# Layer 0's products as sums of seven block products, their sums in two PSUM banks or one, and the row of scores put in order by its transfer

## The chip, the cores and the metric

One core of a Trainium2 chip runs the whole program in one launch. The metric is device time in microseconds. The kernel before takes 2461.74 us, the median of three runs (2460.16 to 2461.83).

## The reference

32 independent graphs of 512 nodes with 256 features go through four graph-attention layers. Each layer normalises x, applies relu to get h, computes a 512x512 matrix of scores, masks it by the graph's adjacency, normalises its rows and mixes the nodes' values. Layer 0 is the one that the change rebuilds most:

```python
h = jnp.maximum(_layernorm(x, axis=-1), 0.0)
# layer 0
mask = jnp.where(dep_adjs == 1, 0.0, NEG).astype(inputs.dtype)
q = jnp.einsum('bnh,hk->bnk', inputs, att_W)
score = jnp.einsum('bnk,bmk->bnm', q, inputs) / jnp.sqrt(jnp.asarray(H, inputs.dtype))
att_adjs = jax.nn.softmax(score + mask, axis=-1)
x = inputs
for W, b in ((W0, b0), (W1, b1)):
    xw = jnp.einsum('bnh,hk->bnk', x, W) + b
    x = jnp.tanh(jnp.einsum('bnm,bmk->bnk', att_adjs, xw))
```

Layers 1 and 2 have scores that are a sum of one number per source and one per target node, through a leaky relu. Layer 3 has full scores again, formed from products of features. All data are float32.

## The kernel before, in words

Every graph is its own chain of operations; P is 128, a graph has NT = 4 tiles of 128 nodes, and features lie in HC = 2 halves of 128. Function `graph` lists the operations of one graph as planner entries: an engine (PE for TensorE, V for VectorE, A for ScalarE, G for GpSimd, D for the transfers on SyncE's queue), a planned cost (how long it holds its engine, and when its result is there), what it comes after, and the buffers that it uses. Class `Plan` then plays all entries of all 32 graphs and of the preparation forward in time. On each engine it takes the ready entry of the best rank, where earlier graphs come first with a distance `apart` between graphs; it tries 32 pairs of such distances and keeps the order that ends first by its own costs. That order is written out as the program, so every engine runs its list in order. An entry starts only when its buffers are free in the plan: 36 pages of SBUF, four value buffers, eight PSUM banks, and five slots, so that at most five graphs are in flight. A slot is taken at a graph's first code operation (L440) or statistics (L461), and is free after the output's store (L987).

Each layer starts with `normed`: statistics (L461, L462), a power on GpSimd (L468), the normalisation (L475), a split of the floats into two planes of 16 bits (L480), a transfer that transposes them (L483), and a copy that joins them into hT, features by nodes (L488).

Layer 0 then has features for all nodes (`features_t`, L513, two banks, evacuated at L517), the values (L682, bias added by L686), the scores (L696, four banks), their Exp straight out of PSUM (L700) and the mask (L703). `attend` (L662) multiplies the scores with the values for two tiles of nodes at a time, in two banks; the last column gives the row sums, of which L711 takes the reciprocal, and L714 applies tanh. L723 repeats the mixing with the result, L741 multiplies with W1, and L745 to L752 finish the layer.

Layers 1 and 2 take scores and values from one product (L596, evacuated by L600 and L603). The scores of the target nodes must become a row that every partition has. For the first and last five graphs TensorE turns them into a bank (L619). For the others `collect` (L624) writes them to DRAM as 128 lines of four numbers, and `spread` (L628) reads them back into a page, for all partitions. `leaky` (L635) adds the source's score and applies the leaky relu, and it reads the row with the two indices exchanged to undo the order in which `collect` wrote it. Exp follows (L639), then the mask (L764 or L791).

Layer 3 computes its features (L838), values (L855), scores (L878) and a further product (L855, for w) by function `seven`: a product of two-by-two blocks done with seven block products instead of eight. `block_sums` (L570) forms the four sums of blocks that some of the products take in place of plain blocks. The four results share partial sums: a bank is evacuated as one result (`write`), the next product is added on top of it in the same bank, the bank is evacuated again as the next result, and so on. The remaining products go to a second and third bank and are added to the results in SBUF (`add`). The weights' seven blocks are made once, by `seven_of`.

The softmax here doesn't subtract the row's maximum and nothing guards it: scores larger than these inputs give would overflow.

## Time and profile before

| | us |
|---|---|
| median of three runs | 2461.74 |
| the profiled execution, whole | 2461.46 |
| its span, first to last instruction | 2459.7 |
| PE busy in the window 401.20 to 2062.00 us | 1641.61 of 1660.80 |
| `row<-sd` to landing (median, 44 transfers) | 3.2 |
| DVE busy in the window 2400 to 2420 us | 19.42 of 20 |

The page's part 1 gives each engine's busy time. The busy time of PE counts pipelined passes from start to modelled end, so it says little on its own. Groups "by line" name the line of the kernel, the engine, the operation, the written and read tiles, the count, the busy time, the mean duration in ns, and the idle time before, with what ended most of it. Windows give busy time of each engine in a stretch. An f32 product is two passes on TensorE, and the counts are of passes.

### The profile page before, as it was taken

Reading aid. Unit: us, or ns where it says so; the run is one execution under the profiler, and the core shown is the slowest. Engines: PE = TensorE matmul, PEld = TensorE weight load, DVE = VectorE, ACT = ScalarE, POOL = GpSimd, SP = SyncE. Lnnn points to the kernel's source line nnn. Section 1 sums busy time; section 2 is a strip of 40 time slices with the busy share of each in tenths; the row PEclk is TensorE's granted clock in tenths of the full one; section 3 lists DMA queues with packets and bytes.
Section 4 is the critical chain, followed back from the end, with each engine's and each line's share of the span. In section 5 each row is a group of like instructions: output and inputs, shape, how many; then the busy total and the mean of one; then the engine's idle time right before and its main releaser. Section 6 shows DMA issues by size and latency. Waiting matters only on the chain.

```text
span 2459.7 us, 33966 instructions
## 1 busy us (share of the span) xinstructions
PE 2407.4 (98%) x10700; PEld 1877.3 (76%) x10700; DVE 1876.2 (76%) x5733; ACT 1742.8 (71%) x3233; POOL 253.8 (10%) x315
## 2 busy tenths in 40 slices
PE   7999999999999999999999999999999999999998
PEld 4678777777777777777777777777777777777877
DVE  5468878777777877787777777777777778756888
ACT  4466777767777777777677777777776777755884
POOL 2001001110010101011101101010011011100110
PEclk9999999999999999999999999999999999999999
DMA  7223333332333322333323333233333343321221
GB/s 178 46 56 82 73 69 82 82 74 54 80 76 82 82 64 64 80 80 82 71 54 81 74 82 82 64 65 80 80 76 70 62 83 81 71 46 22 44 46 41
DMA packets 437204, 175.92 MB, mean 72 GB/s; under 512 B 393408, under 2 KB 410432, under 8 KB 437024
## 3 DMA queue, kind: packets, MB, share of 16 engines
q1 hardware_dynamic: 430976, 154.34, 29.9%
q0 software_dynamic: 5360, 18.75, 2.3%
q8 instruction: 85, 1.39, 0.2%
q14 instruction: 95, 0.78, 0.1%
q10 hardware_dynamic: 688, 0.66, 0.1%
HBM read 64.49 MB, written 16.87 MB: 33 GB/s over the span
## 4 chain that ended last, share of the span: by engine, by line
PE 73%; ACT 17%; DVE 5%; issue 3%; DMA 2%; POOL 0%; SPq 0%; POOLq 0%; ACTq 0%; DVEq 0%
PE bank_a L662 28%; PE bank_v L596 9%; PE bank_z L723 9%; ACT e L635 8%; PE bank_o L741 4%; PE bank_f L513 4%; PE bank_f L838 4%; PE bank_w L855 4%; ACT e L639 3%; PE bank_q L696 3%; PE bank_v L855 3%; PE bank_s L878 3%; ACT xn L475 2%; PE bank_v L682 2%; ACT e L700 1%
## 5 line engine op out<-in xcount | busy, mean ns | idle before, releaser
L662 PE MATMUL bank_a<-v,e 128*128 128x257 f32 (+1 forms) x4096 | 978.0, 381 | 21.8 <-ACT y L714 17.5
L662 PEld LDWEIGHTS bank_a<-v,e 128*128 128x128 f32 x4096 | 757.9, 190 | 199.9 <-issue 68.6
L488 ACT COPY hT<-planesT 128x512 uint16<-128x512 uint16 x512 | 383.2, 767 | 42.1 <-DMA planesT<-planes 41.7
L468 POOL TENSOR_TENSOR rstd<-ve,mhalf 128x2 f32<-128x2 f32 x256 | 215.2, 849 | 1891.7 <-DVE ve L465 1807.6
L475 ACT ACTIVATE xn<-x,off,rstd 128x256 f32<-128x256 f32 x512 | 277.3, 593 | 123.1 <-DVE off L471 119.3
L596 PE MATMUL bank_v<-l_aug,hT 128*128 128x258 f32 x1024 | 251.5, 383 | 3.3 <-ACT r L807 1.7
L480 DVE COPY planes<-xn 128x512 uint16<-128x512 uint16 x512 | 207.9, 422 | 43.8 <-ACT xn L475 24.1
L723 PE MATMUL bank_z<-e,y 128*128 128x512 f32 x512 | 240.6, 592 | 0.0
L696 PE MATMUL bank_q<-fa,hT 128*128 128x512 f32 x512 | 239.3, 592 | 0.0
L596 PEld LDWEIGHTS bank_v<-l_aug,hT 128*128 128x128 f32 x1024 | 192.2, 191 | 35.5 <-issue 3.6
L461 DVE BATCH_NORM_STATS2 st<-x 128x6 f32<-128x256 f32 x512 | 209.0, 408 | 6.6 <-DMA x<-in_x_dram 6.6
L635 ACT ACTIVATE e<-row,sd 128x512 f32<-128x512 f32 x176 | 207.0, 1229 | 0.0
L603 ACT COPY v<-bank_v 128x256 f32<-128x256 f32 x256 | 92.9, 375 | 90.1 <-PE bank_v L596 75.8
L639 ACT ACTIVATE e<-e 128x512 f32<-128x512 f32 x256 | 151.9, 632 | 0.0
L696 PEld LDWEIGHTS bank_q<-fa,hT 128*128 128x128 f32 x512 | 94.9, 190 | 71.4 <-issue 60.8
L723 PEld LDWEIGHTS bank_z<-e,y 128*128 128x128 f32 x512 | 96.5, 190 | 69.1 <-issue 57.9
L885 DVE SCALAR_TENSOR_TENSOR e<-bank_s,v,mask 128x256 f32<-128x256 f32 x256 | 111.1, 476 | 16.5 <-PE bank_s L878 16.3
L682 PE MATMUL bank_v<-w_sb,hT 128*128 128x256 f32 x512 | 121.4, 380 | 0.0
L703 DVE TENSOR_TENSOR e<-e,mask 128x512 f32<-128x512 f32 x128 | 87.5, 688 | 44.0 <-ACT e L700 43.9
L741 PE MATMUL bank_o<-w_sb,zT 128*128 128x256 f32 x512 | 120.4, 379 | 0.0
L513 PE MATMUL bank_f<-hT,att_sb 128*128 128x512 f32 x256 | 119.8, 593 | 0.0
L682 PEld LDWEIGHTS bank_v<-w_sb,hT 128*128 128x128 f32 x512 | 97.1, 191 | 23.9 <-issue 6.1
(134 smaller groups left out, 3702.1 us busy)
## 6 DMA issues: line engine op xcount, KB each, us to landing
adj<-in_adj_dram SPq DMA_DIRECT2D x128, 256.0 KB, 2.9
x<-in_x_dram SPq DMA_DIRECT2D x32, 512.0 KB, 5.1
out_dram<-y POOLq DMA_DIRECT2D x32, 512.0 KB, 4.1
row<-row SPq DMA_DIRECT2D x44, 256.0 KB, 3.7
planesT<-planes SPq DMA_TRANSPOSE x512, 2.4
codeT<-code SPq DMA_TRANSPOSE x128, 2.6
crest<-crest SPq DMA_TRANSPOSE x64, 2.4
raw_w<-in_L_gnn_W_dram POOLq DMA_DIRECT2D x3, 256.0 KB, 7.1
```

Source lines behind the costliest of these rows:

```text
L468: nc.gpsimd.tensor_tensor(T[f"rstd{l}"][:, two(g)], T[f"ve{l}"][:, two(g)], mhalf[:, two(g)], ALU.pow)
L475: nc.scalar.activation(T[f"xn{l}"][:, t, :], T["x"][:, t, :], AF.Relu, bias=T[f"off{l}"][:, t : t + 1], scale=T[f"rstd{l}"][:, t : t + 1])
L488: nc.scalar.copy(bits[:, :, :, t * P : (t + 1) * P], T[f"planesT{l}_{t}"].rearrange("p (b c) n -> p b c n", b=2))
L513: nc.tensor.matmul(T[key], w_sb[:, c, k * P : (k + 1) * P], T[f"hT{l}"][:, c, :], start=(c == 0), stop=(c == HC - 1))
L596: nc.tensor.matmul(T[key][:, :cols], T[f"hT{l}"][:, c, t * P : (t + 1) * P], w_aug[:, c, :], start=(c == 0), stop=(c == HC - 1))
L635: nc.scalar.activation(e(l, c).rearrange("q (t p) -> q t p", t=NT), row, AF.Prelu, bias=T[f"sd{l}"][:, 1, c : c + 1], alpha=ALPHA)
L639: nc.scalar.activation(e(l, c), e(l, c), AF.Exp, scale=sign)
L662: nc.tensor.matmul(T[keys[j]][:, : LEAD + H + 1 - lead], e(l, c)[:, t * P : (t + 1) * P], T[f"v{l}"][:, c, lead:], start=(c == 0), stop=(c ...
L682: nc.tensor.matmul(T[key][:, j * H : (j + 1) * H], T["hT0"][:, c, t * P : (t + 1) * P], w0_sb[:, c, :], start=(c == 0), stop=(c == HC - 1))
L696: nc.tensor.matmul(T[key], T["hT0"][:, k, c * P : (c + 1) * P], T["fa0"][:, k, :], start=(k == 0), stop=(k == HC - 1))
L723: nc.tensor.matmul(T[f"bank_z{k}"], T["y0"][:, c, k * P : (k + 1) * P], e(0, c), start=(c == 0), stop=(c == NT - 1))
L741: nc.tensor.matmul(T[key][:, j * H : (j + 1) * H], T["zT"][:, k, t * P : (t + 1) * P], w1_sb[:, k, :], start=(k == 0), stop=(k == HC - 1))
```

## The change

Layer 0's three products (features, values, scores) go through `seven` as well. Its weights W0 and att_W are loaded into pages and turned into seven blocks by `seven_of`, as layer 3's are. `block_sums` forms hs0 from hT0, and fs0 from the features. Scores now come block by block: the block that is whole after one evacuation gets its Exp out of PSUM as before; the other three are copied out, get the further products added, and get their Exp in place.

`seven` itself, for layers 0 and 3, uses two banks instead of three, and one bank in two halves where a block product is at most 256 columns wide (`beside`: features and values of layer 0, features and w of layer 3). Its fifth product now waits for the fourth and for the addition of the second.

The row of scores of layers 1 and 2 is put in node order by `collect`, which writes single numbers to their places in DRAM, and L635 reads it straight. Planned costs change with it: 5000 in place of 3500 ns for `collect`'s landing, 629 in place of 570 ns for the leaky relu of the row out of SBUF, 334 in place of 395 and 602 in place of 640 for additions out of PSUM.

```diff
-V_SUM, V_INTO, V_BLOCK = (334.0, 425.0), (640.0, 730.0), (790.0, 880.0)
+V_SUM, V_BLOCK = (334.0, 425.0), (790.0, 880.0)
...
-D_OUT, D_SPREAD = (550.0, 3500.0), (550.0, 4500.0)
+D_OUT, D_SPREAD = (550.0, 5000.0), (550.0, 4500.0)
...
-    att_sb, w0_sb, w1_sb = (tile_of(n, H) for n in ("att_sb", "w0_sb", "w1_sb"))
-    l3_w1s, m3 = (tile_of(n, HALF, 7) for n in ("l3_w1s", "m3"))
+    w1_sb = tile_of("w1_sb", H)
+    att_s, w0_s, l3_w1s, m3 = (tile_of(n, HALF, 7) for n in ("att_s", "w0_s", "l3_w1s", "m3"))
...
-    nc.scalar.dma_start(out=w0_sb, in_=rows_of(w0))
-    nc.scalar.dma_start(out=att_sb, in_=rows_of(att_w))
+    w0_sb, att_sb = raw("raw9"), raw("raw10")
     nc.scalar.dma_start(out=b0_sb, in_=line_of(b0))
+    for n, dst, w, key in (("att", att_s, att_w, "raw10"), ("w0", w0_s, w0, "raw9")):
+        a = prepare("A", (500.0, 4000.0), [], lambda w=w, key=key: nc.scalar.dma_start(out=raw(key)(), in_=rows_of(w)), key)
+        ready[n] = seven_of(raw(key), dst, HALF, [a], key)
...
-        def features_t(l, hs, w_sb, ready):
...
-                key = f"bank_f{l}{k}"
-                def product(k, key):
-                    for c in range(HC):
-                        nc.tensor.matmul(T[key], w_sb[:, c, k * P : (k + 1) * P], T[f"hT{l}"][:, c, :],
-                                         start=(c == 0), stop=(c == HC - 1))
...
-                    nc.scalar.copy(T[f"fa{l}"][:, k, :], T[key])
...
-                a = op("PE", pe(n512=4), hs + ready, partial(product, k, key), key, f"hT{l}")
-                done.append(op("A", A_COPY, [a], partial(evacuate, k, key), key, f"fa{l}"))
...
-        def seven(key, cost, after, keys, work, write, add):
...
-            first = times(1, 0, True)
-            c11 = out(write, 0, 0, 0, first)
-            c12 = out(write, 0, 1, 0, times(6, 0, False, c11))
-            c22 = out(write, 1, 1, 0, times(7, 0, False, c12))
-            c21 = out(write, 1, 0, 0, times(4, 0, False, c22))
-            c11 = out(add, 0, 0, 1, times(2, 1, True, first), c11)
-            c22 = out(add, 1, 1, 2, times(5, 2, True, first), c22)
-            c12 = out(add, 0, 1, 2, times(3, 2, False, c22), c12)
+        def seven(key, cost, after, keys, work, write, add, beside=0):
...
+            p, q = f"bank_{key}p", f"bank_{key}{'p' if beside else 'q'}"
+            def times(x, bank, start, fresh, *wait):
+                return op("PE", cost, after(x) + list(wait), lambda: work(x, T[bank][:, start:], fresh), bank, *keys)
+            c11 = write(0, 0, p, 0, [times(1, p, 0, True)])
+            two = times(2, q, beside, not beside, c11)
+            c12 = write(0, 1, p, 0, [times(6, p, 0, False, c11)])
+            c22 = write(1, 1, p, 0, [times(7, p, 0, False, c12)])
+            four = times(4, p, 0, False, c22)
+            c21 = write(1, 0, p, 0, [four])
+            c11 = add(0, 0, q, beside, [two, c11])
+            c22 = add(1, 1, q, beside, [times(5, q, beside, True, four, c11), c22])
+            c12 = add(0, 1, q, beside, [times(3, q, beside, False, c22), c12])
             return {(0, 0): c11, (0, 1): c12, (1, 0): c21, (1, 1): c22}
...
-                line.append(dram.tile([P, NT], F32, tag=f"row_{T.places['slot']['number']}", name=f"row{l}_{b}"))
-                nc.sync.dma_start(out=line[0], in_=T[f"sd{l}"][:, 0, :])
+                line.append(dram.tile([N], F32, tag=f"row_{T.places['slot']['number']}", name=f"row{l}_{b}"))
+                nc.sync.dma_start(out=line[0].rearrange("(t p) -> p t", p=P), in_=T[f"sd{l}"][:, 0, :])
...
-                if turned:
-                    row = T[key].rearrange("q (t p) -> q t p", t=NT)
-                else:
-                    row = T[key][:, 0, :].rearrange("q (p t) -> q t p", t=NT)
-                nc.scalar.activation(e(l, c).rearrange("q (t p) -> q t p", t=NT), row, AF.Prelu,
-                                     bias=T[f"sd{l}"][:, 1, c : c + 1], alpha=ALPHA)
+                row = T[key] if turned else T[key][:, 0, :]
+                nc.scalar.activation(e(l, c), row, AF.Prelu, bias=T[f"sd{l}"][:, 1, c : c + 1], alpha=ALPHA)
...
-            ls = [op("A", A_PRELU, [a], partial(leaky, c), key, f"e{l}_{c // 2}") for c in range(NT)]
+            ls = [op("A", A_PRELU if turned else A_PRELU2, [a], partial(leaky, c), key, f"e{l}_{c // 2}") for c in range(NT)]
...
+        def features_t(l, right_after, right, w, ready, bias=None):
+            def work(x, p, fresh):
+                nc.tensor.matmul(p[:, : N // 2], w[:, x - 1, :], right(x), start=fresh, stop=True, skip_group_check=True)
...
+                def emit():
+                    if bias is None:
+                        nc.scalar.copy(block(i, l_), T[key][:, : N // 2])
+                    else:
+                        nc.scalar.activation(block(i, l_), T[key][:, : N // 2], AF.Identity, bias=bias[:, i : i + 1])
+                return op("A", A_HALF if bias is None else A_HALF_BIAS, after, emit, key, f"fa{l}")
...
+            def add(i, l_, key, start, after):
+                return op("V", V_SUM, after, lambda: nc.vector.tensor_tensor(
+                    block(i, l_), block(i, l_), T[key][:, start : start + N // 2], ALU.add), key, f"fa{l}")
+            done = seven(f"f{l}", pe(n256=2), lambda x: right_after(x) + ready, (f"hT{l}", f"hs{l}"), work, write, add,
+                         beside=N // 2)
+            return list(done.values())
...
-        qs = features_t(0, hs, att_sb, [])
-        vs = []
...
-            a = op("PE", pe(n256=8), hs[two(g)], partial(values, g, key), key, "hT0")
-            vs += [op("V", V_ADD, [a], partial(biased_v, g, j, key), key, "v0") for j in range(2)]
-        es = []
-        for c in range(NT):
...
-                    nc.tensor.matmul(T[key], T["hT0"][:, k, c * P : (c + 1) * P], T["fa0"][:, k, :],
-                                     start=(k == 0), stop=(k == HC - 1))
...
-                nc.scalar.activation(e(0, c), T[key], AF.Exp, scale=float(H) ** -0.5)
...
-            def masked0(c):
-                nc.vector.tensor_tensor(e(0, c), e(0, c), T["mask0"][:, c, :], ALU.mult)
-            a = op("PE", pe(n512=4), qs, partial(similar, c, key), key, "hT0", "fa0")
-            a = op("A", A_COPY, [a], partial(exp0, c, key), key, f"e0_{c // 2}")
-            es.append(op("V", V_MASK, [a, m0], partial(masked0, c), "mask0", f"e0_{c // 2}"))
+        right_after, right = block_sums("hs0", "hT0", lambda j, l, T=T: T["hT0"][:, j, half(l)], hs, left=False)
+        qs = features_t(0, right_after, right, att_s, ready["att"])
...
+        def write_v0(i, l, key, start, after):
+            return op("V", V_SUM, after, lambda: nc.vector.tensor_tensor(
+                block_v0(i, l), two_tiles(key, start, HALF),
+                b0_sb[:, i * HALF : (i + 1) * HALF].unsqueeze(1).to_broadcast([P, 2, HALF]), ALU.add), key, "v0")
+        def add_v0(i, l, key, start, after):
+            return op("V", V_SUM, after, lambda: nc.vector.tensor_tensor(
+                block_v0(i, l), block_v0(i, l), two_tiles(key, start, HALF), ALU.add), key, "v0")
+        vs = seven("v0", pe(nt=4), lambda x, after=right_after: after(x) + ready["w0"], ("hT0", "hs0"),
+                   partial(by_nodes, w0_s, right), write_v0, add_v0, beside=N // 2)
+        vs = [tuple(vs.values())] * NT
...
+        def scores0(right, left, x, p, fresh):
+            for j in range(2):
+                nc.tensor.matmul(p[:, j * N // 2 : (j + 1) * N // 2], right(x)[:, j * P : (j + 1) * P], left(x),
+                                 start=fresh and j == 0, stop=True, skip_group_check=True)
...
+        def write_q(i, l, key, start, after):
+            if (i, l) == (1, 0):
+                return op("A", A_COPY, after, partial(exp0, i, l, key), key, f"e0_{l}")
+            return op("A", A_COPY, after, lambda: nc.scalar.copy(block_e0(i, l), two_tiles(key, 0, N // 2)), key, f"e0_{l}")
+        def add_q(i, l, key, start, after):
+            a = op("V", V_MASK, after, lambda: nc.vector.tensor_tensor(
+                block_e0(i, l), block_e0(i, l), two_tiles(key, 0, N // 2), ALU.add), key, f"e0_{l}")
+            exps.append(op("A", A_EXP, [a], partial(exp0, i, l), f"e0_{l}"))
+            return exps[-1]
+        def masked0(i, l):
+            nc.vector.tensor_tensor(block_e0(i, l), block_e0(i, l), T["mask0"][:, two(l), half(i)], ALU.mult)
+        exps = []
+        qb = seven("q0", pe(n256=4), lambda x, right_after=right_after, left_after=left_after: right_after(x) + left_after(x),
+                   ("hT0", "hs0", "fa0", "fs0"), partial(scores0, right, left), write_q, add_q)
+        es = {il: op("V", V_MASK, [a, m0], partial(masked0, *il), "mask0", f"e0_{il[1]}") for il, a in qb.items()}
+        es = [(es[0, c // 2], es[1, c // 2]) for c in range(NT)]
...
-        fb = seven("f3", pe(n256=2), lambda x: right_after(x) + ready["m3"], ("hT3", "hs3"), features3, write_f, add_f)
...
+        ks = features_t(3, right_after, right, m3, ready["m3"], bias=l3_u2)
...
-            return op("V", V_INTO, after, lambda: nc.vector.tensor_tensor(s(), s(), two_tiles(key, N // 2), ALU.add),
+            return op("V", V_MASK, after, lambda: nc.vector.tensor_tensor(s(), s(), two_tiles(key, 0, N // 2), ALU.add),
...
-        wb = seven("w3", pe(nt=4), lambda x: right_after(x) + ready["w3"], ("hT3", "hs3"), partial(by_nodes, l3_w1s), write_w, add_w)
...
+        wb = seven("w3", pe(nt=4), lambda x: right_after(x) + ready["w3"], ("hT3", "hs3"), partial(by_nodes, l3_w1s, right), write_w, add_w, beside=N // 2)
```

`two_tiles`, `by_nodes` and the feature functions of layer 3 move ahead of layer 0 so that both use them, with the start column in the bank as a further argument.

## The prediction

> **What bounds the kernel now.** I read the page first, for the engines' shares:
>
> ```profile
> PE 2407.4 (98%) x10700; PEld 1877.3 (76%) x10700; DVE 1876.2 (76%) x5733; ACT 1742.8 (71%) x3233; POOL 253.8 (10%) x315
> ```
>
> PE looks full, but a busy PE may still not issue at its peak. So I took the chain that ended last and looked for its rhythm (start, length, what):
>
> ```profile
> 1187.65 4.33 PE bank_a L662 x20
> 1262.94 4.33 PE bank_a L662 x20
> ```
>
> The same piece returns every 75.29 us: that is one graph in the steady state, and 32 graphs of it are 2409 of the 2459.7 us of span. Then the PE timeline, for the distance from one pass to the next (start, length, group, xcount; an f32 product is two passes):
>
> ```profile
> 34.14 6.17 PE L696 MATMUL bank_q<-fa,hT 128*128 128x512 f32 x14
> 1288.93 1.02 PE L838 MATMUL bank_f<-hs,m 128*128 128x256 f32 x4
> 1284.12 0.61 PE L855 MATMUL bank_w<-l_w1s,hT 128*128 128x128 f32 x4
> ```
>
> A group's length less the mean length of one of its passes (592, 380 and 275 ns in the groups by line), over the passes less one, gives (6.17 - 0.592) / 13 = 0.429 us for a pass of 512 columns, 0.215 for 256 (other groups give 0.217; I take 0.216) and 0.112 for 128. By counts per graph from the groups: attention 128 passes of 0.217, the scored values of layers 1 and 2 32 of 0.218, z 16 of 0.429, o 16 of 0.216, layer 3's block products 14 and 28 of 0.216 and 56 of 0.112, layer 0's 16 + 8 of 0.429 (q and features) and 16 of 0.216 (values). That is 27.8 + 7.0 + 6.9 + 3.5 + 15.3 + 10.3 + 3.5 = 74.2 us of 75.29. So PE issues without a break but for 1.1 us per graph. The waits and the timelines of PE and DVE say where that 1.1 us is:
>
> ```profile
> PE bank_a L662 <- ACT y L714: 17.5, 20, 0.9
> 1099.55 1.78 PE L662 MATMUL bank_a<-v,e 128*128 128x257 f32 x7 [0.90 <-ACT y L714]
> ```
>
> It is one wait per graph: layer 0's tanh, which frees an attention bank, is late because its reciprocal (L711) stood behind DVE work without a gap since 1093.9, and before that ACT did two row operations of L635. The other engines in five steady periods (length, then PE, PEld, DVE, ACT, POOL busy; two of the five shown):
>
> ```profile
> 675.30:750.60 75.30, 74.44 (x332) 58.12 (x331) 58.47 (x179) 55.68 (x102) 7.83 (x9) 1.00 0.36 74
> 750.60:825.90 75.30, 74.41 (x332) 58.06 (x331) 58.45 (x179) 55.67 (x102) 7.83 (x9) 1.00 0.34 74
> ```
>
> DVE has 16.8 us free in a period, ACT 19.6. The rows that the change touches or copies:
>
> ```profile
> L635 ACT ACTIVATE e<-row,sd 128x512 f32<-128x512 f32 x176 | 207.0, 1229 | 0.0
> L635 ACT ACTIVATE e<-bank_r,sd 128x512 f32<-128x512 f32 x80 | 52.4, 693 | 14.0 <-PE bank_r L619 13.9
> L893 DVE TENSOR_TENSOR e<-e,bank_s 128x512 f32<-128x512 f32 x96 | 64.7, 681 | 3.0 <-PE bank_s L878 2.9
> L846 DVE TENSOR_TENSOR fa<-fa,bank_f 128x256 f32<-128x256 f32 x96 | 40.0, 419 | 28.4 <-PE bank_f L838 24.0 <-ACT fa L841 4.2
> L838 PE MATMUL bank_f<-hs,m 128*128 128x256 f32 x256 | 72.4, 380 | 1.0 <-ACT fa L841 0.9
> ```
>
> The last one matters most: layer 3 runs the same chains of product, evacuation and next product today, and PE loses 1.0 us to them in the whole run, since other graphs fill the gaps.
>
> **What the Trainium skill says.** "Perfetto Trace Analysis", Identifying the Most-Contended Engine: matmul busy share is a poor measure of how near PE is to its limit. Hence the count of passes above; it agrees here, because passes fill 98.5% of the period. "SBUF — State Buffer", Specifications (TRN2): lines of 16 bytes, of which an access should hit two elements for full rate. The row is read with a step of 16 bytes today, one element a line, and the trace agrees: 1229 ns against 693 for the ordered row in PSUM and 716 for a plain SBUF Prelu (L924). "DMA: Bandwidth & Descriptors", Specifications: below 512 B a transfer does not reach line rate. The trace of before has no DMA with runs of 4 B.
>
> **The change, part by part.**
>
> PE, per graph, layer 0. Removed: 8 x 0.429 + 16 x 0.216 + 16 x 0.429 = 13.75 us. Added: 14 x 0.216 + 28 x 0.112 + 28 x 0.216 = 12.21 us. That is 1.54 us less, 49.3 us over 32 graphs. PE sets the end, so this counts in full if no new wait appears. Pass rates at 256 and 128 columns are those of layer 3, so I see no doubt about them.
>
> DVE, per graph. Layer 0's four masks and four bias additions stay in number and size. Added: eight block sums (L570 form, 418 ns), three sums each for features and values (419), three for scores (681): 8 x 0.418 + 6 x 0.419 + 3 x 0.681 = 7.9 us. 58.5 becomes 66.4 of a period of 73.8, or 90%. Cover: DVE's 16.8 us of idle time, of which 7.4 would remain. Issued back to back such sums take 0.34 and 0.60, so the floor is 6.6 us.
>
> ACT, per graph. Features: four half copies (376 as L865) for two whole ones (585), +0.3; scores: three copies more (585) and three Exps from SBUF (632) in place of PSUM (591), +1.9; eight leaky rows at about 720 in place of 1229 in the 22 middle graphs, -4.1. Net -1.9 us; ACT goes to 53.7 of 73.8. It is no bound; its worth is earlier masks of layers 1 and 2, and so perhaps the 1.1 us wait.
>
> The row's way. The write to DRAM is 512 runs of 4 B in place of 128 of 16 B. Queue 1 spent 29.9% of 16 x 2459.7 us on 430976 packets, 27 ns each, so 384 more over 16 engines are 0.7 us, twice that at worst: 3.2 us to landing becomes 4 to 4.6. The read-back waits for it on SP's queue (58.3 us in 20 times now), with transposes behind; at most 1.4 x 44 = 62 us more of waiting there, in a graph that is one of five. I cost it at nothing; without that cover it would be 1 us per layer and graph, 44 us.
>
> Banks and latency. With two banks (or one in two halves) product 5 now waits for product 4 and for the first addition. Layer 3's feature chain runs from 1282.8 to 1293.4 today; I estimate 2 to 4 us more for each of its chains, and for layer 0 about layer 3's 42 us from hT to scores against 33 now (1064 to 1097). A slot (five in all) is taken by the first L440 at 997.6 and freed after the store at 1366.8, but layer 0's statistics of that graph begin only at 1043: some 45 us of reserve against 15 to 20 more. Nothing, unless that is used up.
>
> Start and tail. The weights' blocks are two more sets of DVE work of 1.7 us (the sum of m's rows, L342 to L347), in a stretch where DVE is busy 16.0 of 20 us, and the first graphs' chains have little to fill them: +3, between 0 and 8. At the end DVE is at 19.3 and 19.4 of 20 us; layer 3's longer chains lie bare there: +2, between -2 and 6.
>
> The 1.1 us wait: the plan by which the order was made puts L635 at 570 ns (A_PRELU), and from SBUF it takes 1229; the new order counts 629 for about 720, so work of the middle graphs will come nearer to its planned time. But DVE gets fuller. From all of the wait gone (20 x 1.1 = -22) to as much again (+22); I take 0.
>
> Sum, against the profiled execution (2461.5 us: span 2459.7 and 1.8 around it; the median, 2461.7, is the same): 2461.5 - 49.3 + 3 + 2 = **2417 us**, its own range 2396 to 2437.
>
> **Rivals.** (A) DVE backlog costs one more wait per graph of the kind at 1099, 1.1 us in some 26 graphs: 2446. For it: that wait already comes from DVE work without a gap, and 7.9 us more comes in. Against: planned order can shift work between five graphs. (B) The ordered row takes the wait away and the start costs nothing: 2417 - 22 - 3 = 2392. For it: two L635 of 2.26 us stand at the head of the chain into that wait. Against: DVE is fuller. (C) Slower: DVE at 90% delays evacuations, sums and reciprocals in its queue, and PE runs out of ready products in the stretch where one graph's layer 0 meets another's layer 3, both in chains. Before's densest stretch, 2360 to 2435 us, has DVE at 69.5 of 75.3 and PE at only 70.3, that is 5 us lost; against it, few graphs are left there. With 5 us lost per steady period instead of 1.1 a graph takes 72.7 + 5 = 77.7, 2.4 us over now in some 26 graphs: 2461.5 + 62 = 2524. It decides from 1.1 + 1.5 = 2.6 us of PE idle per period on. (D) The gain is there and given back to within the noise, at 2.6 us idle: 2461.
>
> **How the numbers follow.** Forecast 0.52, A 0.17, B 0.09, C 0.18, D 0.04. The range 2388 to 2460 takes in the forecast, A and B and a part of D and leaves about 2 in 10 out. A measurement tells 0.2% (5 us) from no change: faster 0.78, same 0.04, slower 0.18.
>
> **What would show it.** Right: a period of about 73.8 us in the chain; 332 PE passes per period become 362; DVE near 66 busy, the row operations near 720 ns; PE waits of about 1 us per graph. Wrong: PE busy below 71 of a period with waits on DVE sums or ACT writes of the seven-product chains (C), or store-to-store times set by the slots. Layer-0 products that wait at their banks would show the two-bank chain mis-costed.

## The result, and the profile after

The changed kernel takes 2762.18 us (median of 4 runs, 2759.41 to 2765.04) against 2461.78 us for the kernel before (2460.16 to 2462.91). The ratio is 1.1221, with a 95% interval of 1.1201 to 1.124: 300 us slower. The prediction said 2417 us, and its range ended at 2460.

The profiled execution took 2759.41 us, with a span of 2757.6 us. The page's first part gives the engines' busy time, share of the span and instructions (after):

```profile
span 2757.6 us, 36523 instructions
PE 2462.7 (89%) x11660; PEld 2043.8 (74%) x11660; DVE 2051.3 (74%) x6289; ACT 1717.9 (62%) x3393; POOL 242.2 (9%) x315
```

PE went from 98% to 89%: the span grew by 298 us and PE's busy time by 55 us, so PE stood idle for most of the growth. DVE is at 74%, so the engine that got the new sums is not full. Now the costliest groups of the same page, those of the row and of the turned features (line engine op, out<-in, count | busy, mean ns | idle before, and what ended it):

```profile
L490 ACT COPY hT<-planesT 128x512 uint16<-128x512 uint16 x512 | 381.1, 769 | 293.2 <-DMA planesT<-planes 292.3
L616 ACT ACTIVATE e<-row,sd 128x512 f32<-128x512 f32 x176 | 118.5, 710 | 6.7 <-DMA row<-row 6.7
```

The row operation dropped from 1229 to 710 ns, as forecast. But the copy of the turned features, L490, which the diff does not touch, now stands 292 us behind a DMA transpose. In the waits (engine, line, what it waited for: us, times, longest) PE comes next in that line (after):

```profile
ACT hT L490 <- DMA planesT<-planes: 292.3, 85, 12.4
...
PE bank_v L580 <- ACT hT L490: 162.9, 24, 9.9
...
PE bank_v0p L685 <- DVE v L697: 68.8, 17, 8.4
```

The first of them in before, where the copy is L488:

```profile
ACT hT L488 <- DMA planesT<-planes: 41.7, 57, 3.6
```

In time order the chain of waits shows where such a transpose stands (start, length, what; after):

```profile
1008.88 12.66 DMA planesT<-planes
...
1022.38 2.09 PE bank_v L580 x4
...
1028.06 12.44 DMA row<-sd
1040.59 3.36 DMA row<-row
...
1095.08 12.39 DMA planesT<-planes
...
1183.51 12.13 DMA planesT<-planes
1196.48 2.09 PE bank_v L580 x4
```

In the chain of before, where PE and ACT alternate, no wait for a DMA of this kind is longer than 4.3 us. The write of the row takes 12.44 us (3.2 before), and three transposes take 12 us each; the median of a transpose before was 2.4 us. The time between the last two of them, 88.43 us, has taken the place of the 75.29 that a graph took before. What went onto the queue just ahead of the late transposes is in SP's timeline (start, length of the issue, what; after):

```profile
1007.81 0.38 SPq L608 DMA_DIRECT2D row<-sd  x1
1008.29 0.50 SPq L430 DMA_DIRECT2D x<-in_x_dram  x1
1008.88 3.03 SPq L485 DMA_TRANSPOSE planesT<-planes  x2
...
1183.03 0.38 SPq L608 DMA_DIRECT2D row<-sd  x1
1183.51 1.44 SPq L485 DMA_TRANSPOSE planesT<-planes  x1
```

At 1007.81 the row is written (L608); 0.5 us later the next load of x is issued and 1.1 us later two transposes, and the copy that waits for them starts only at 1021.57. At 1183.03 the order is the same without the load of x, and the transpose is as late, so the load is not what holds it. What ACT and PE do meanwhile (start, length, ..., idle time before in brackets), first ACT, then PE (after):

```profile
1021.57 0.76 ACT L490 COPY hT<-planesT 128x512 uint16<-128x512 uint16 x1 [9.19 <-DMA planesT<-planes]
```

```profile
1186.27 1.03 PE L580 MATMUL bank_v<-l_aug,hT 128*128 128x258 f32 x4
...
1196.48 2.09 PE L580 MATMUL bank_v<-l_aug,hT 128*128 128x258 f32 x4 [6.99 <-ACT hT L490]
```

Two things are to be seen here. PE is idle for 6.99 us, and the four passes that follow take 2.09 us where four passes of the same form took 1.03 us ten microseconds earlier. The granted clock says why (stretch; its length, then PE, PEld, DVE, ACT, POOL busy; granted clock, DMA share, GB/s; after):

```profile
1183.50:1189.40 5.90, 5.90 (x34) 5.19 (x32) 5.40 (x19) 2.60 (x6) 0.18 (x1) 1.00 1.51 79
1194.10:1200.90 6.80, 4.42 (x10) 3.53 (x11) 1.49 (x6) 2.47 (x5) 1.37 (x2) 0.50 0.69 152
```

It was whole before the pause and is half for the 6.8 us that begin in the pause. The Trainium skill ("TensorE: Matmul & The Clock Gate", Part 1: The HAM clock gate) says that the clock is halved after an idle window and comes back after some microseconds of activity; this trace agrees. So the mean granted clock is 0.952 here and 0.998 before.

To get a sum out of this I took the distance of every PE pass to the next and subtracted what its group usually takes. What is over is idle time and slow passes. By stretches of the span (us), for before, after and the first two experiments below (e1 and e2):

| kernel | passes at usual distance | before the first pass | over, 0 to 400 | over, middle | over, last 400 | after the last pass |
|---|---|---|---|---|---|---|
| before | 2392.3 | 11.0 | 8.5 | 25.8 | 14.1 | 7.8 |
| after | 2347.7 | 12.1 | 25.9 | 349.3 | 14.6 | 7.8 |
| row's way back (e1) | 2347.9 | 12.1 | 22.1 | 38.7 | 16.6 | 8.0 |
| row's way alone (e2) | 2393.3 | 11.9 | 10.1 | 257.1 | 17.1 | 7.8 |

The block products thus save nearly what they should, and the middle loses some 320 us more than before. Past 400 us, 252 gaps in after hold 296 us, and 35 gaps of over 3 us hold 237 of these (before has no such gap); 416 passes at half speed hold 69 us more.

### The profile page after: what moved, and what is told of

The parts are those of the page before. It is cut to its first block, busy times and chain, and to the rows that moved or that the text cites. A ratio compares the mean times of both kernels' runs of the same rounds, so it can differ in the third digit from the quotient of the medians.

```text
span 2757.6 us, 36523 instructions
## 1 busy us (share of the span) xinstructions
PE 2462.7 (89%) x11660; PEld 2043.8 (74%) x11660; DVE 2051.3 (74%) x6289; ACT 1717.9 (62%) x3393; POOL 242.2 (9%) x315
## 4 chain that ended last, share of the span: by engine, by line
PE 64%; DMA 19%; ACT 7%; DVE 6%; issue 3%; POOL 0%; SPq 0%; ACTq 0%; POOLq 0%; DVEq 0%
PE bank_a L642 28%; DMA planesT<-planes 17%; PE bank_z L757 8%; PE bank_v L580 5%; PE bank_o L775 4%; PE bank_v0p L685 3%; PE bank_w3p L685 3%; PE bank_s3p L889 3%; PE bank_s3q L889 2%; PE bank_f0p L659 2%; ACT hT L490 2%; PE bank_q0q L712 2%; PE bank_f3p L659 2%; PE bank_q0p L712 2%; ACT xn L477 1%
## 5 line engine op out<-in xcount | busy, mean ns | idle before, releaser
L490 ACT COPY hT<-planesT 128x512 uint16<-128x512 uint16 x512 | 381.1, 769 | 293.2 <-DMA planesT<-planes 292.3
L580 PE MATMUL bank_v<-l_aug,hT 128*128 128x258 f32 x1024 | 286.9, 411 | 163.0 <-ACT hT L490 162.9
L470 POOL TENSOR_TENSOR rstd<-ve,mhalf 128x2 f32<-128x2 f32 x256 | 206.4, 818 | 2191.4 <-DVE ve L467 2114.3
L580 PEld LDWEIGHTS bank_v<-l_aug,hT 128*128 128x128 f32 x1024 | 204.9, 206 | 200.7 <-ACT hT L490 169.2
L584 DVE COPY sd<-bank_v 128x2 f32<-128x2 f32 x256 | 37.4, 153 | 208.8 <-ACT v L587 187.7
L619 ACT ACTIVATE e<-e 128x512 f32<-128x512 f32 x256 | 150.4, 624 | 0.0
L720 ACT ACTIVATE e<-e 128x512 f32<-128x512 f32 x96 | 60.4, 630 | 121.4 <-DVE e L729 121.4
L896 DVE SCALAR_TENSOR_TENSOR e<-bank_s3p,v,mask 128x256 f32<-128x256 f32 x256 | 111.3, 476 | 19.4 <-PE bank_s3p L889 18.5
L616 ACT ACTIVATE e<-row,sd 128x512 f32<-128x512 f32 x176 | 118.5, 710 | 6.7 <-DMA row<-row 6.7
L685 PE MATMUL bank_v0p<-w_s,hT 128*128 128x128 f32 x384 | 66.2, 299 | 61.6 <-DVE v L697 61.4
L775 PEld LDWEIGHTS bank_o<-w_sb,zT 128*128 128x128 f32 x512 | 97.6, 192 | 19.4 <-ACT zT L761 5.4
L685 PEld LDWEIGHTS bank_v0p<-w_s,hT 128*128 128x128 f32 x384 | 59.6, 209 | 70.4 <-DVE v L697 67.1
## 6 DMA issues: line engine op xcount, KB each, us to landing
out_dram<-y POOLq DMA_DIRECT2D x32, 512.0 KB, 12.5
```

The lines of the kernel that those rows point to most:

```text
L470: nc.gpsimd.tensor_tensor(T[f"rstd{l}"][:, two(g)], T[f"ve{l}"][:, two(g)], mhalf[:, two(g)], ALU.pow)
L490: nc.scalar.copy(bits[:, :, :, t * P : (t + 1) * P], T[f"planesT{l}_{t}"].rearrange("p (b c) n -> p b c n", b=2))
L580: nc.tensor.matmul(T[key][:, :cols], T[f"hT{l}"][:, c, t * P : (t + 1) * P], w_aug[:, c, :], start=(c == 0), stop=(c == HC - 1))
L619: nc.scalar.activation(e(l, c), e(l, c), AF.Exp, scale=sign)
L685: nc.tensor.matmul(p[:, j * k : (j + 1) * k], right(x)[:, j * P : (j + 1) * P], w[:, x - 1, :], start=fresh and j == 0, stop=True, skip_gr ...
L775: nc.tensor.matmul(T[key][:, j * H : (j + 1) * H], T["zT"][:, k, t * P : (t + 1) * P], w1_sb[:, k, :], start=(k == 0), stop=(k == HC - 1))
```

## The experiments

Theory after the result: the row's write, 512 runs of 4 B, holds up the transposes behind it. Rival: the seven-product chains with two banks (the prediction's C), which run late and let everything behind slide.

**One part undone, one part alone.** First, after with the old way of the row: 16 B lines in DRAM, read with a step of 16 B by the leaky operation, the plan's old costs.

```diff
-                nc.sync.dma_start(out=line[0].rearrange("(t p) -> p t", p=P), in_=T[f"sd{l}"][:, 0, :])
+                nc.sync.dma_start(out=line[0], in_=T[f"sd{l}"][:, 0, :])
...
-                row = T[key] if turned else T[key][:, 0, :]
+                    row = T[key][:, 0, :].rearrange("q (p t) -> q t p", t=NT)
```

> The changed kernel with the row of scores handled as before: written as 128 lines of four numbers, read by L635's counterpart with exchanged indices, planned costs of the two back. Theory R (the write of the row in runs of 4 B occupies the DMA engines, and the transposes behind it come late): near the forecast of the rest, 2400 to 2440 us, transposes to landing near 2.4 us. Rival S (layer 0's chains of seven products, with DVE work and bank waits, starve PE): stays above 2650 us. Rival M (both): between 2450 and 2650 us.

Measured: 2448.27 us (2447.37 to 2450.62), ratio to before 0.9944 (0.9928 to 0.9961). All of the loss and more is gone, though the time lies 8 us above the range expected of the theory: a part of the change still costs something, which the last experiments look for. Page and waits of this run (row's way back):

```profile
PE 2388.1 (98%) x11660; PEld 1988.9 (81%) x11660; DVE 2052.3 (84%) x6289; ACT 1811.5 (74%) x3393; POOL 250.4 (10%) x315
```

```profile
PE bank_w L309 <- DMA raw_w<-in_L_gnn_W_dram: 12.4, 1, 12.4
PE bank_v0p L689 <- DVE v L706: 7.6, 20, 1.0
...
PE bank_v L580 <- ACT hT L490: 1.6, 3, 1.1
```

The wait for the turned features, 162.9 us in after, is 1.6 us here, and the 68.8 us that layer 0's values waited for their first biased block (L697 there, L701 here) are 1.1: so that wait in after came from the late transposes too, further along the chain of operations. What is left of a wait for the new chains is small: a product of layer 0's values that waits at its bank for an addition (L706), 20 times, for at most 1.0 us. So products with seven blocks and fewer banks are by themselves a small gain, some 14 us or 0.6%.

Second, before with nothing but the row's way changed:

```diff
-                nc.sync.dma_start(out=line[0], in_=T[f"sd{l}"][:, 0, :])
+                nc.sync.dma_start(out=line[0].rearrange("(t p) -> p t", p=P), in_=T[f"sd{l}"][:, 0, :])
```

> The kernel before with the row part of the change alone. Theory R: 2700 to 2800 us, with waits of about 10 us for the transposes, about 44 of them. Rival S: 2440 to 2465 us. Rival M: 2500 to 2650 us.

Measured: 2697.79 us (2694.32 to 2699.45), ratio 1.0952 (1.0936 to 1.0969). That is just under the expected span, but the direction is clear: the row's way alone loses some 234 us. The copies wait in the same way as in after (waits, row's way alone):

```profile
ACT hT L488 <- DMA planesT<-planes: 354.1, 116, 9.1
```

The median from issue to landing of a transpose is 2.5 us in this run and 2.4 before (the profile of after gives none): a median over 512 transposes hides those that stand behind one of 44 writes. Taken apart, the 86 transposes of this run that were issued while a row's write was under way landed after 9.2 us in the median, the other 426 after 2.4.

**The write alone.** These two runs change the order of instructions too, since the plan's costs changed. So I left before as it is, its plan included, and added a second write of the same numbers after each of the 44, to a place that nobody reads. All the following spare writes are work that the reference doesn't need.

```diff
                 nc.sync.dma_start(out=line[0], in_=T[f"sd{l}"][:, 0, :])
+                spare = dram.tile([N], F32, tag=f"spare_{T.places['slot']['number']}", name=f"spare{l}_{b}")
+                nc.sync.dma_start(out=spare.rearrange("(t p) -> p t", p=P), in_=T[f"sd{l}"][:, 0, :])
```

> The kernel before, in its order, where each of the 44 writes of the row is followed by a second write of the same numbers in runs of 4 B to a spare place in DRAM that nobody reads. Theory R: the transposes behind it are late although nobody waits for the spare write, so 2650 to 2800 us. Rival W (what costs is only that the row itself arrives late): within 10 us of 2462. A plain cost by packets (27 ns each over 16 engines, 0.9 us a write): at most 40 us more, 2500 us.

Measured: 2611.54 us (2603.78 to 2618.64), ratio 1.0603 (1.0578 to 1.0629): less than expected, yet 149 us for 44 small writes. In the list of DMAs (out<-in, engine, count, KB each, median us from issue to landing) of this run:

```profile
row<-row SPq DMA_DIRECT2D x44, 256.0 KB, 9.7
...
codeT<-code SPq DMA_TRANSPOSE x128, 5.6
...
spare<-sd SPq DMA_DIRECT2D x44, 2.0 KB, 11.6
```

The spare write lands after 11.6 us. The row's read-back, which the same instructions issue as before and which is now behind it, lands after 9.7 us where it took 3.7, and half of the codes' transposes after 5.6 us or more where it was 2.6. (These medians rest on the transfers whose landing the profile tells, 14 of the 44 spare writes.) What ACT waits for in this run (waits, spare write):

```profile
ACT e L637 <- DMA row<-row: 103.1, 20, 7.4
ACT hT L488 <- DMA planesT<-planes: 77.6, 65, 9.2
```

The row itself comes late here too, and that wait is the longer one, while in after it is only 6.7 us. So the spare write makes late what is near it, and which transfer then costs most differs with the order of the kernel. The control is the same spare write in lines of 16 B:

```diff
-                spare = dram.tile([N], F32, tag=f"spare_{T.places['slot']['number']}", name=f"spare{l}_{b}")
-                nc.sync.dma_start(out=spare.rearrange("(t p) -> p t", p=P), in_=T[f"sd{l}"][:, 0, :])
+                spare = dram.tile([P, NT], F32, tag=f"spare_{T.places['slot']['number']}", name=f"spare{l}_{b}")
+                nc.sync.dma_start(out=spare, in_=T[f"sd{l}"][:, 0, :])
```

> As e3, but the spare write goes in 128 lines of 16 B, as the row's own write does before. Theory R (the 4 B runs are what costs): within 15 us of 2462. If any further write between the transposes costs as much: as e3.

Measured: 2464.54 us, ratio 1.0009 (1.0 to 1.0017), landing 3.1 us. A further DMA on the queue costs next to nothing; its form does.

**Number, size or place of the runs?** A quarter of the runs, 128 of 4 B, still one next to the other (512 B in all):

```diff
+                spare = dram.tile([P], F32, tag=f"spare_{T.places['slot']['number']}", name=f"spare{l}_{b}")
+                nc.sync.dma_start(out=spare.rearrange("(p o) -> p o", o=1), in_=T[f"sd{l}"][:, 0, 0:1])
```

> The kernel before, in its order, with a spare write of 128 runs of 4 B (one number of each partition) after each of the 44 writes of the row; nobody reads it. In e3 512 such runs cost 149 us. Theory N (the cost goes by the number of runs): a quarter, 37 us, about 2500 us. Theory F (any write in runs of 4 B has a fixed cost): 2580 to 2620 us. Theory L (runs that fall into the same short stretch of DRAM hinder one another): between 2465 and 2510 us.

Measured: 2591.87 us (2587.33 to 2603.49), ratio 1.0529 (1.0503 to 1.0555), landing 9.5 us. The number of runs doesn't decide (theory N): a quarter of them costs nearly as much. Theory L, which expected at most 2510 us, missed as well; only theory F met the number. Then all 512 runs of 4 B again, but each 512 B from the next:

```diff
+                spare = dram.tile([P, NT, P], F32, tag=f"spare_{T.places['slot']['number']}", name=f"spare{l}_{b}")
+                nc.sync.dma_start(out=spare[:, :, 0], in_=T[f"sd{l}"][:, 0, :])
```

> As e3, 512 runs of 4 B, but each to its own place 512 B from the next. Theory N: as e3, 2600 to 2620 us. Theory L: well under e3, 2465 to 2520 us. Theory F: as e3.

Measured: 2466.4 us, ratio 1.0015 (1.0008 to 1.0022), landing 4.5 us. The same number of runs of the same 4 B is harmless if they lie apart. So neither the size of a run, as theory F had it after the run before, nor the number is the cause by itself; it takes runs that lie close to each other in DRAM. That is theory L's idea, without the small cost that it gave to 128 runs. Two more pitches, with 128 runs (`[P, 2]` and `[P, 4]` in place of `[P]`, written in column 0):

> As e5 (128 runs of 4 B after each write of the row, 2592 us), but each run 8 B from the next instead of 4. Theory K (what costs is how many runs fall into one short stretch of DRAM, one after the other): about half of e5's 128 us, 2510 to 2545 us, and its landing between 5 and 8 us against 9.5. Theory X (only neighbouring runs that touch, without a gap, hinder one another): 2463 to 2470 us.

> As e5, each run 16 B from the next. Theory K: a quarter or less, since e4's lines of 16 B, just as far apart, cost 2 us: 2463 to 2490 us, landing 3 to 5 us. If the length of 4 B alone were what costs, as e5: about 2590 us.

| spare write | landing, us | time, us | ratio to before |
|---|---|---|---|
| 128 runs of 4 B, pitch 4 B | 9.5 | 2591.87 | 1.0529 |
| 128 runs of 4 B, pitch 8 B | 4.9 | 2474.9 (2471.72 to 2477.38) | 1.004 (1.0026 to 1.0054) |
| 128 runs of 4 B, pitch 16 B | 3.6 | 2465.89 | 1.0007 (0.9999 to 1.0015) |
| 128 lines of 16 B | 3.1 | 2464.54 | 1.0009 |

Over the 3.1 us of the last row the landing is later by 6.4, 1.8 and 0.5 us: it falls faster than with the inverse of the pitch, which would give 3.2 and 1.6 us at 8 and 16 B. At 8 B both expected ranges were missed: the time is far from half the cost (theory K), and a little above no cost (theory X). 1.8 us of delay cost 11 us of time, 0.25 us a write, and 6.4 us cost 128, 2.9 us a write; so, as an estimate from these numbers, 1.5 to 3.5 us of such a delay are covered in this plan. What in the memory makes neighbouring runs so slow is not shown by these runs. That writes to one short stretch of DRAM are taken one after the other would fit the direction of all the landings, the 512 apart among them, but not by itself the fall to less than a third at twice the pitch; it stays a guess.

**Does another queue help?** If the write only blocks its own queue, it should do no harm on another one. The row's write of after on ScalarE's queue, then on GpSimd's (the plan's op "D" becomes "A" or "G"):

```diff
-                nc.sync.dma_start(out=line[0].rearrange("(t p) -> p t", p=P), in_=T[f"sd{l}"][:, 0, :])
+                nc.scalar.dma_start(out=line[0].rearrange("(t p) -> p t", p=P), in_=T[f"sd{l}"][:, 0, :])
```

> The changed kernel with the row's write in runs of 4 B issued on ScalarE's queue instead of SyncE's. Theory Q (only what stands behind it on the same queue is late): the transposes go on as before, 2420 to 2480 us; the row itself still lands late, 9 to 13 us. Theory E (the DMA engines, or the memory behind them, are held for all queues): 2650 to 2800 us, as the changed kernel's 2762.

> As e13, on GpSimd's queue. Theory Q: 2420 to 2500 us (GpSimd also computes rstd, which may come later). Theory E: 2650 to 2800 us.

Measured: 2659.3 us (2650.72 to 2662.31), ratio 1.0787 (1.0768 to 1.0807), and 2681.96 us (2674.55 to 2688.99), ratio 1.0876 (1.0846 to 1.0906). That recovers 103 and 80 of the 314 us that separate after from the row's way back; both times lie in theory E's range. Why it recovers that much is not shown (the order of the program changes too). The wait, with the write on ScalarE's queue:

```profile
ACT hT L490 <- DMA planesT<-planes: 292.7, 113, 9.9
```

The copies wait as long in all for the transposes, still on SP's queue, as before the move (292.3). With the write on GpSimd's queue the landings can be taken apart: the 56 transposes issued while a row's write was under way landed after 9.2 us in the median, the other 456 after 2.4. The store of the output, on GpSimd's queue in every kernel, shows it from the other side. In after, 18 of the 32 stores were issued within 1.5 us of a row's write; those with a known landing took 12.5 to 13.5 us, the others 3.7 in the median. In the kernel of the next experiment, where the row goes out in lines of 16 B, 20 stores stand as close to a write and take 4.0 to 5.3 us. So the write holds up what the queues share (theory E). The Trainium skill says what that may be ("DMA: Bandwidth & Descriptors", Issuing engines are not separate DMA queues): DMAs of every issuing engine end on the same 16 DMA engines. These runs agree, but they do not tell the DMA engines from the memory behind them.

**The order without the small runs.** If the gain of an ordered row is to be had otherwise, the lines of 16 B can stay in DRAM, and one GpSimd copy per row puts the numbers in order inside SBUF:

```diff
+            def sort_row():
+                nc.gpsimd.tensor_copy(T[key][:, 1, :].rearrange("q (t p) -> q t p", t=NT),
+                                      T[key][:, 0, :].rearrange("q (p t) -> q t p", t=NT))
...
-                row = T[key] if turned else T[key][:, 0, :]
+                row = T[key] if turned else T[key][:, 1, :]
...
+                a = op("G", (900.0, 1000.0), [a], sort_row, key)
```

> The changed kernel with the row written and read back as before (16 B lines), and put in order by one copy on GpSimd inside its page, so that ScalarE reads it straight and its planned cost is the changed kernel's. GpSimd is 10% busy. If the slow row on ScalarE costs PE something in the steady state: 5 to 25 us under e1's 2448. If ScalarE has room for it: within 5 us of 2448. [...]

Measured: 2426.25 us (2424.97 to 2428.18), ratio 0.985 (0.9835 to 0.9865). The chain's rhythm and the copy (GpSimd copy):

```profile
1600.70 7.80 PE bank_a L647 x36
1673.79 7.80 PE bank_a L647 x36
```

```profile
L615 POOL COPY row<-row 128x512 f32<-128x512 f32 x44 | 51.1, 1162 | 236.5 <-DMA row<-row 159.6 <-PE bank_v0p L690 31.5 <-PE bank_q0q L717 22.6
```

A graph takes 73.1 us here, and the copy costs an engine that is mostly idle 1.2 us a row. Against the row's way back, 22 us are gained: PE's idle time in the middle falls from 38.7 to 18.6 us, less than the 25.8 of before. So a leaky operation at 710 ns (the plan's order changes with its planned cost) does take waits away, as rival B held, but only 7 us below before.

**What is left: banks or start?** Three banks for each chain again, as layer 3 had them before, first with the row's way back, then, with the GpSimd copy, in the 22 middle graphs alone (e11):

```diff
-            p, q = f"bank_{key}p", f"bank_{key}{'p' if beside else 'q'}"
...
+            c11 = out(add, 0, 0, 1, times(2, 1, True, first), c11)
+            c22 = out(add, 1, 1, 2, times(5, 2, True, first), c22)
+            c12 = out(add, 0, 1, 2, times(3, 2, False, c22), c12)
```

> e1 with the seven block products in three banks, as layer 3 had before, for layers 0 and 3. If the two-bank chains make the new PE waits (0.5 us a graph more than before, and some 12 us in the first 300 us): 2420 to 2440 us. If they come from VectorE's longer queue: within 5 us of 2448. If eight banks are too few for three per product: slower than 2455.

> e7 (row put in order by GpSimd, 2426 us) with three banks per product in the 22 middle graphs and two or one in the first and last five. In e8 three banks took PE's waits in the middle from 39 to 20 us, but the start rose by 14. If the chains' banks are what makes the remaining waits in the middle (19 us in e7): 2410 to 2422 us. If DVE's queue makes them: within 4 us of 2426. If eight banks are short: slower than 2430.

Measured: 2443.76 us (2439.57 to 2446.84), ratio 0.9919 (0.9904 to 0.9934), and 2431.3 us (2427.13 to 2433.5), ratio 0.9862 (0.9849 to 0.9875). In the first, by the same count of PE's distances, the middle loses 20.4 in place of 38.7 us, but the first 400 us lose 35.8 in place of 22.1. In all, the first run is 4.5 us under the row's way back with two banks, not under the 2440 that were expected if the banks made the waits. The second is 5 us slower than with two banks, at the edge of what was expected if eight banks are short; by the same count its middle loses as much as with two banks, and its first 400 us some 9 us more. With the row in order, the fewer banks aren't what holds this kernel back.

The start is next. In the first five graphs there is little other work to fill a chain of seven products, so these graphs got the plain products of before, with the weights kept in their raw pages (with the GpSimd copy; `features_plain` and the `values` and `similar` that go with it are before's):

```diff
+        if b < FLIGHT:
+            qs = features_plain(hs)
...
+        else:
+            right_after, right = block_sums("hs0", "hT0", lambda j, l, T=T: T["hT0"][:, j, half(l)], hs, left=False)
```

> e7 with layer 0 of the first five graphs done by plain products as before; the seven-product way from the sixth graph on. These five graphs have 7.7 us more of PE passes. If the bare chains of the first graphs cause the 13.5 us that PE waits more in the first 400 us: 2416 to 2422 us. If the start is longer for another cause (weights' blocks, order of the preparation): 2430 to 2436 us.

Measured: 2416.92 us (2416.69 to 2418.68), ratio 0.9808 (0.9795 to 0.9821): the fastest of all kernels run here, 47 us under the 2464.12 of before that ran beside it. PE's loss in the first 400 us falls from 22.0 to 10.9 us, for 6.5 us more of passes. The stretch from 0 to 400 us (us; PE, PEld, DVE, ACT, POOL busy; granted clock, DMA share, GB/s), with plain products in five graphs and, below, with the GpSimd copy alone:

```profile
0.00:400.00 400.00, 380.02 (x1640) 291.51 (x1640) 284.13 (x914) 251.67 (x488) 50.90 (x73) 1.00 0.35 81
```

```profile
0.00:400.00 400.00, 371.52 (x1769) 305.03 (x1770) 310.16 (x983) 254.28 (x503) 50.01 (x72) 1.00 0.36 80
```

PE is busy for 8.5 us more, and DVE has 26 us less to do in that time. Whether the chains' own length or these sums on DVE held PE up at the start is not told apart by this run.

## Why the prediction was wrong

The step that failed is "The row's way". It priced 512 runs of 4 B by the mean packet time of queue 1, 27 ns: 0.7 us, twice that at worst, 4 to 4.6 us to landing. Measured are 10.5 to 12.4 us. A mean over 430976 packets of other forms says little about neighbouring runs of 4 B, and not even the packets' own records do: in after, behind the write issued at 1028.06, the trace holds 528 packets of 4 B between 1028.9 and 1029.4, recorded at 7 to 9 ns each, after which no packet of any kind ends for 3.2 us; the write's landing is seen only at 1040.50. By the recorded time my price was not too low; the cost lies in what follows.

The second half of the same step failed too: "I cost it at nothing", because the row belongs to one graph in five. The row itself is mostly covered: ACT stood idle before the leaky operations for only 6.7 us in the whole run, though the chain passes through one such write at 1028. But the transposes behind the write are those of another graph, and all graphs wait for theirs. The step named them as queued behind, and gave them no price beyond "1 us per layer and graph, 44 us". That the delay was 7 to 9 us in place of about 1 turned 44 us into 314: (2762.18 - 2448.27) / 44 = 7.1 us for each write. (Against the GpSimd copy, which has the same ordered row without the slow write, it is 336 us.)

The other terms, by the table of PE's distances (row's way back against before, unless said):

| term of the sum | forecast, us | measured, us | from |
|---|---|---|---|
| PE passes of 32 graphs | -49.3 | -49.2 | 2347.9 - 2392.3 = -44.4, without 4.8 of slower passes at the start |
| start | +3 (0 to 8) | +19.5: 13.6 idle, 1.1 before the first pass, 4.8 slower passes | 0 to 400, first pass, L326 |
| waits of the middle | 0 (-22 to +22) | +12.9; with the ordered row by GpSimd -7.2 | middle |
| end | +2 (-2 to 6) | +2.5 | last 400 |
| the row's way | 0 | +314 (taken as the difference) | after against row's way back |

- The passes: right. In a steady period their usual distances sum to 72.52 us, 1.57 less than before, where 1.54 was forecast. The 4.8 us are the preparation's products (L326), which run slower there: 652 ns in the mean in place of 452 for 256 columns.
- The row operation: 710 ns for "about 720".
- DVE and the two banks: right in direction. DVE is busy for 1377.89 of 1600 us from 400 to 2000 us in the row's way back, 86% where 90% was forecast. The chains do cost a new wait per graph (at most 1.0 us on L706's addition), and the old one at L714 is gone. Rivals A and C rested on these; C's "slower" came true by another cause, and the row's way back rules C out as that cause.
- The start: mis-sized by 16.5 us. The estimate counted the weights' blocks as DVE work and touched the first graphs' chains in half a sentence. The run with plain products in five graphs shows that the seven-product way of the first graphs, chains and sums together, is the larger part: 11 of the 13.6 us of idle time go with it.

With these sizes the sum is 2461.5 - 49.2 + 19.5 + 12.9 + 2.5 = 2447 for the row's way back (2448 measured), and 2761 with the row's 314 (2762 measured; since the 314 is a difference of these two times, this last step proves nothing by itself). That the best kernel here stands at the forecast 2417 is chance: it has another way of ordering the row and other products at the start.

The warning was within reach. The prediction had itself cited a lower limit for fast transfers and said that no DMA of the trace had runs of 4 B. That holds for the writes; the preparation does read four short vectors in elements of 4 B (2.0 and 1.0 KB, landing after 4.3 to 7.3 us), but amid large loads that land as late. A form that the trace doesn't have should have got its upper bound from the whole transfer and not from its packets: four times the runs, so at worst four times the landing, 4 x 3.2 = 12.8 us. (The runs show that the number isn't the reason, so it is luck that this bound would have held the 12.4.) With that bound on every transfer behind the write, the range could not have ended at 2460.

## What to carry to other kernels

Reorder in SBUF, as the GpSimd copy does, or let the engine read with a step, but don't write DRAM in neighbouring runs of 4 B: the write of 2 KB lands 7 to 9 us later here and holds up the DMAs of other queues for about that long. For a DMA in a form that the trace has not yet, ask first who stands behind it in any queue, and try the one form by a spare write in the untouched kernel before it is built in. And look at the longest wait and at the chain, not only at the median landing of a group, since 86 slow transfers vanish in 512, as with the row's way alone.

## What the runs showed that was not expected

- 512 runs of 4 B side by side land after 10.5 to 12.4 us, 128 of them after 9.5; at a pitch of 8 B, 4.9; of 16 B, 3.6; 512 of them at 512 B apart, 4.5 us. Closeness counts far more than the number.
- The delay reaches transfers on other queues: moving the write away from the transposes' queue brought back only 80 to 103 of 314 us, and with the write on GpSimd's queue the transposes issued on SP's queue meanwhile landed after 9.2 us in place of 2.4.
- After 6.99 us without a product, four passes took 2.09 us in place of 1.03. In after, slow passes of this kind add 69 us to 296 us of gaps, so the waits of PE cost there about a quarter more than their length.
- GpSimd orders a row of 128x512 f32 that is read with a step of 16 B in 1162 ns, once; ScalarE loses 1229 - 710 = 519 ns in each of the four reads of that row.
